# A decoder layer on one core: a new opening, a buffer moved, and a new table of order offsets

## The chip, the core and the metric

The kernel runs on one NeuronCore of a Trainium2 chip. The core has a matrix engine (TensorE; PE in the profile, with its weight loads shown apart as PEld), a vector engine (VectorE, DVE), a scalar engine for activations and copies (ScalarE, ACT), a general engine (GpSimd, POOL) and a queue engine that here only issues transfers (SyncE, SP). Each engine executes its own list of instructions strictly in the order of that list and waits at its head for what it needs. ScalarE and GpSimd can issue transfers as well. Matrix products write to PSUM; everything else lives in SBUF. The metric is device time in microseconds (us) of the whole program; 1557.06 us is the median of three runs before the change, and lower is better.

## What is computed

A decoder layer in float32 for 4 sequences (B) of 512 tokens and width 512, in three parts, each followed by "add to the residual and layer-normalise":

```
x = layernorm(x + attention(x))   # 8 differential heads: p1 - lam * p2, 4 key/value groups, causal
x = layernorm(x + mamba(ctx) )    # in-projection of a 256-wide context, 4-tap convolution, silu,
                                  # x-projection to dt/B/C, a scan of 16 states over 512 steps, times silu(x)
x = layernorm(x + ffn(x))         # shared gated unit + 16 experts in a latent of 128, top 8 of 16 weighted
```

The second part's in-projection, convolution, x-projection and scan depend only on the context `ctx`, so they can run from the beginning beside the attention. The feed-forward part first projects the tokens to the 128-wide latent (`xl`) and to 16 gate values, and every expert is computed for every token with a weight that may be zero.

## The kernel before

**Who orders the work.** The body does not issue instructions at once. Every `nc.<engine>.<op>` call is recorded by `Notes.note` (L208) as a step with a key, a time-like number: a stage's own due time (`nc.key`) plus an offset from the table `SHIFT` (L23 to L39), looked up by the name of the tile written and the initial of the engine ("y.v": the tile `y` on VectorE; "cT.s": the tile `cT` from SyncE or ScalarE). When all is recorded, `Notes.order` (L253) plays the program through once with fixed costs per step: whenever an engine is free in that play, it takes the ready step with the lowest key. A step is only taken if its buffer is free, and VectorE operations that read two SBUF operands are kept apart in time from wide GpSimd additions. `Notes.trace` emits the steps in the order found, all from one line, so that nearly every row of the profile says L358. The order is thus fixed before the run; if on the chip an input comes later than in that play, the engine waits even if later steps of its list could run.

**The opening.** L455 to L475 load, all from SyncE's queue: small vectors (`bq`, `cw`, `cb`), the in-projection weights `w_in` in two halves and the first sequence's context `cT0` in two halves, then `xT0` (the transposed tokens), the first key, query and value weights (`wk`, `wq`, `wv`), `w_xp`, the lambda vectors `lt`, and more small ones. With key 0, L477 to L487 turn the lambda vectors into `nlam` (tiles `lp`, `ls`) and `a_neg` into its negated exponential on VectorE and ScalarE. L490 to L496 load the four residuals `res[b]` (1 MB each) and the output bias `obb`, and let GpSimd add `obb` to each residual, one 128 by 2048 addition for each sequence.

**The context part.** `scan(b)` (L647) has four products of two steps each into `ps_in` (8 products; a float32 product is two MATMUL records in the trace, so 16 records), a copy of each to `xm`, one ScalarE and three VectorE operations of the convolution into `y`, a sigmoid `sgc` on ScalarE over each pair of blocks, and `y * sgc` on VectorE. `ps_x` needs both halves of `y`; its copy `xd` goes out to memory, comes back as broadcast rows `bc`, and feeds products `ps_dt` with only 16 rows of weights. Then come 16 state steps of two halves with a scan instruction each, accumulated to memory by GpSimd's transfers `y<-h`. For the first sequence all of this has key 0; `ps_qk`, `ps_v` and `s` products of the first attention unit follow.

**Attention and experts.** 16 attention units (4 groups by 4 sequences), each with about 73.8 us of key. Then `experts(b)` for each sequence: gate and latent products `ps_gate`, `xr` (the latent by tokens, copied from PSUM by ScalarE), four transposes `pt_l` into `xl`, the top-8 weights, the shared unit (`pg_s`, `ph_s`), and 16 experts of `pg`, `ph`, `pa`, fed by `wb`, `xw` and `ht`, two buffers each. SBUF tiles come from tagged sets: "pT" has 2 buffers and "c2" has 6 (`C2`). `wb`, `xw`, `ht` are all from "c2", as are `w_in`, `xm`, `xd`, `w_dt` earlier on; `xr`, `wT`, `aT`, `sg` and `relu_s` are from "pT".

Of the kernel before, what the change touches and what calls it, by code (L numbers as in the profile page):

```python
# [19 lines left out]
P = 128  # L20
ENGINES = ("tensor", "vector", "scalar", "gpsimd", "sync")

SHIFT = {  # L23
    "aT.s": 15.4, "a_neg.s": 12.1, "a_neg.v": -7.8, "bc.s": 7.4, "bq.s": -3.3, "bvb.s": -2.6, "cT.s": -3.5,
    "cf.v": -1.7, "cw.s": -2.2, "da.g": -4.8, "da.s": -1, "db.s": 4.2, "dsk.s": 2.1, "dt.s": -2.1, "dt.v": -7.7,
    "du.v": 21.2, "e.s": 7.6, "e.v": -2.1, "gb.s": -1.2, "h.v": -4.3, "ht.v": -6.5, "kT.s": 3.9, "l.v": 2.1,
    "ln_mv.v": -14.5, "ln_nb.v": -33.8, "ln_rs.g": -2.5, "ln_st.v": 4.7, "ln_ve.v": -21.4, "lo.v": 12.6, "lp.v":
    2.2, "ls.s": -1.8, "ls.v": -6.6, "lt.s": 3, "m.v": -3.7, "ms.v": -4.3, "nlam.v": -8.1, "o.s": -12.8, "oT.s":
    0.7, "obb.s": 17, "ow.s": -1.2, "pT.s": -2.7, "pa.t": 1, "pg.t": -2.1, "pg_s.t": -8.4, "ph.t": 2.8, "ph_s.t":
    3.2, "po.t": -7.2, "pr.s": -9.5, "pr.v": -13, "ps_dt.t": -0.1, "ps_gate.t": -18.9, "ps_in.t": -1.8,  # L30
    "ps_out.t": 5.1, "ps_qk.t": 1.3, "ps_v.t": 2.1, "ps_x.t": 12.8, "ps_y.t": 2.9, "pt.t": -0.3, "pt_o.t": 2.7,
    "pt_w.t": -7.1, "pt_x.t": 1.5, "pt_y.t": -5.9, "qT.s": 0.6, "relu.s": 20.5, "relu_s.s": -3.8, "res.g": -0.4,
    "res.s": -5.4, "res.v": -1.8, "rp.v": -16.4, "rs.g": 6.5, "rs.v": -12.2, "s.t": 0.9, "sc.v": 4, "sg.s": -1.5,
    "sg.v": 4.3, "sgc.s": 3.9, "sh.v": 7.5, "sp.v": 15.5, "sq.s": -16.2, "sub.s": -33.5, "sub.v": -9.9, "v.v":
    1.5, "w.s": 6.4, "wT.s": -1.1, "w_dg.s": 0.9, "w_dt.s": 6.5, "w_e.s": 23.5, "w_in.s": -30.8, "w_s.s": -0.3,
    "w_u.s": -4.7, "w_xp.s": 1.8, "wb.s": 10.2, "wq.s": 2.4, "wv.s": 5.9, "x2T.s": -13.1, "xd.s": 17.9, "xl.s":
    2.9, "xm.g": 1.7, "xm.s": 7.8, "xr.s": -1, "xw.v": 3.9, "y.g": -4.6, "y.s": 7.9, "y.v": -9.9, "yb.s": 5.6,
    "yb.v": 2.7,
}  # L39
B, S, HID = 4, 512, 512  # L40
NT = S // P
# [3 lines left out]
CTX, DI, NST, DTR, KC = 256, 512, 16, 16, 4  # L45
ND = DI // P
LAT, FH, NE, SCALE = 128, 256, 16, 2.5
NEG = -1e30
C2 = 6
# [322 lines left out]
def decoder_kernel(  # L372
# [11 lines left out]
    sb = Pool(ctx.enter_context(tc.tile_pool(name="sb", bufs=1)))  # L384
    ps = Pool(ctx.enter_context(tc.tile_pool(name="ps", bufs=1, space=PSUM)), psum=True)
    dram = Pool(ctx.enter_context(tc.tile_pool(name="scratch", bufs=1, space=DRAM)))

    ident = fixed.tile([P, P], F32, tag="ident", name="ident")
# [10 lines left out]
    nc = Notes(real)  # L399

    def load(shape, src, tag, name=None, bufs=1, most=0):
        t = sb.tile(shape, tag, name or tag, bufs, most)
        nc.sync.dma_start(out=t, in_=src)
        return t

    def small(shape, tag, bufs=8):
        return sb.tile(shape, tag, tag, bufs)
# [35 lines left out]
    def load_q(g):  # L443
        return [
            load([P, 4, 256], wqkvT[:, k : k + 256].rearrange("(c p) n -> p c n", p=P), "wq", "wq", 2)
            for k in (g * 512, g * 512 + 256)
        ]
# [4 lines left out]
    def load_cT(b):  # L452
        return load([P, 2, S], ctxT[b].rearrange("(c p) t -> p c t", p=P), "h", "cT", 5)

    nc.key = -40.0  # L455
    bq = load([P, 32], bqkv, "bq")
    cw = load([P, ND, KC], convw, "cw")
    cb = load([P, ND], convb, "cb")
    w_in, cT0 = [], sb.tile([P, 2, S], "h", "cT", 5)
    for c in range(2):  # L460
        w_in.append(load([P, DI], inT[c * P : (c + 1) * P, :], "c2", "w_in", C2))
        nc.sync.dma_start(out=cT0[:, c, :], in_=ctxT[0, c * P : (c + 1) * P, :])
    xT0 = sb.tile([P, 4, S], "t8", "xT")
    wk0 = load_k(0)
    for c in range(4):
        nc.sync.dma_start(out=xT0[:, c, :], in_=xT[0, c * P : (c + 1) * P, :])
    wq0 = load_q(0)
    wv0 = load_v(0)
    w_xp = load([P, ND, 48], xpT.rearrange("(c p) n -> p c n", p=P), "w_xp")
    lt = load([P, 2, 2, HD], lam4.partition_broadcast(P).rearrange("p (a c d) -> p a c d", a=2, c=2), "qT", "lt", 2)  # L470
    sub = load([P, 2], subln, "sub")
    w_dt = load([DTR, DI], dtT, "c2", "w_dt", C2)
    db = load([P, ND], dtb, "db")
    dsk = load([P, ND], dskip, "dsk")
    a_neg = load([P, ND, NST], alog, "a_neg")  # L475
# [4 lines left out]
    lp = sb.tile([P, 2, HD], "o", "lp", 2)  # L480
    ls = sb.tile([P, 2], "ls")
    nlam = sb.tile([P, 1], "nlam")
# [8 lines left out]
    res = [sb.tile([P, NT, HID], f"res{b}") for b in range(B)]  # L491
    obb = load([P, HID], ob.partition_broadcast(P), "oT", "obb", 2)
# [13 lines left out]
    def layernorm(src, dst, tiles=range(NT)):  # L506
        st = small([P, NT, 6], "ln_st", 2)
        mv = small([P, NT, 2], "ln_mv", 2)
        ve = small([P, NT], "ln_ve", 2)
        rs = small([P, NT], "ln_rs", 2)  # L510
        nb = small([P, NT], "ln_nb", 2)
        k = slice(tiles[0], tiles[-1] + 1)
        for i in tiles:
            nc.vector.bn_stats(out=st[:, i, :], in_=src[:, i, :])
            nc.vector.bn_aggr(out=mv[:, i, :], in_=st[:, i, :])
        nc.vector.tensor_scalar(ve[:, k], mv[:, k, 1], EPS, None, ALU.add)
        nc.gpsimd.tensor_tensor(rs[:, k], ve[:, k], mhalf[:, k], ALU.pow)
        nc.vector.scalar_tensor_tensor(nb[:, k], mv[:, k, 0], -1.0, rs[:, k], ALU.mult, ALU.mult)
        for i in tiles:
            nc.scalar.activation(  # L520
                dst[:, i, :], src[:, i, :], AF.Identity, bias=nb[:, i : i + 1], scale=rs[:, i : i + 1]
            )


    qk_scale = HD ** -0.5
# [204 lines left out]
    w_dg = sb.tile([P, 4, LAT + NE], "w_dg")  # L730
    nc.sync.dma_start(out=w_dg[:, :, :LAT], in_=wdT.rearrange("(c p) n -> p c n", p=P))
    nc.sync.dma_start(out=w_dg[:, :, LAT:], in_=wgT.rearrange("(c p) n -> p c n", p=P))
    gb = load([P, NE], gbias.partition_broadcast(P), "gb")
    w_s = sb.tile([P, 2, 4, FH], "t8", "w_s")
# [3 lines left out]
    w_u = load([P, HID], wuT, "wq", "w_u", 2)  # L738
# [6 lines left out]
    def experts(b):  # L745
        T = t_expert(b)
        nc.key = T - LEAD[b]
        if b:
            yb = [load([P, 2, S], y_d[b][:, k : k + 2, :], "o", "yb", 2) for k in (0, 2)]
            yb = [yb[d // 2][:, d % 2, :] for d in range(ND)]  # L750
        else:
            yb = [load([P, S], y_d[b][:, d, :], "c2", "yb", C2, 4) for d in range(ND)]
        nc.key = max(T - LEAD[b] + 10.0, nc.key + 5.0)
        for i in range(NT):
            sg = sb.tile([P, HID], "pT", "sg", 2)
# [3 lines left out]
        for i in range(NT):  # L759
            pt = ps.tile([P, S], "tr", "pt_y", 1)  # L760
# [4 lines left out]
        x2T = [sb.tile([P, 2, S], t, "x2T") for t in ("wk", "wv")]  # L765
        x2T = [x2T[c // 2][:, c % 2, :] for c in range(4)]
        for c in range(4):
            pt = ps.tile([P, S], "tr", "pt_x", 1)
# [3 lines left out]


        nc.key += 10.0
        pls, xr = [], sb.tile([P, NT, LAT], "pT", "xr", 2)
        for k in range(2):
            pl = ps.tile([P, 2, 256], "mm", "ps_gate", 3)
            for i in range(2):
                t = 2 * k + i
                for c in range(4):  # L780
                    nc.tensor.matmul(
                        pl[:, i, : LAT + NE], lhsT=x2T[c][:, t * P : (t + 1) * P], rhs=w_dg[:, c, :],
                        start=(c == 0), stop=(c == 3),
                    )
            pls.append(pl)
        pr = small([P, NT, NE], "pr", 1)
# [4 lines left out]
        pt = ps.tile([P, S], "tr", "pt_l", 1)  # L791
        for i in range(NT):
            nc.tensor.transpose(pt[:, i * P : (i + 1) * P], xr[:, i, :], ident)
        xl = sb.tile([P, S], "kT", "xl", 2)
        nc.scalar.copy(xl, pt)
        sc = small([P, NT, NE], "sc", 1)
        nc.vector.tensor_tensor(sc, pr, gb.repeat(1, [P, NT, NE]), ALU.add)
        m8 = small([P, NT, 8], "m8", 1)
        rp = small([P, NT, NE], "rp", 1)
        for i in range(NT):  # L800
            nc.vector.max(out=m8[:, i, :], in_=sc[:, i, :])
            nc.vector.match_replace(
                out=rp[:, i, :], in_to_replace=m8[:, i, :], in_values=sc[:, i, :], imm_value=-3e38
# [3 lines left out]
        sp = small([P, NT], "sp", 2)  # L807
# [3 lines left out]
        pt = ps.tile([P, S], "tr", "pt_w", 1)  # L811
        for i in range(NT):
            nc.tensor.transpose(pt[:NE, i * P : (i + 1) * P], pr[:, i, :], ident)
        wT = sb.tile([NE, S], "pT", "wT", 2)
# [5 lines left out]
        sh = sb.tile([P, 2, S], "v", "sh", 2)  # L820
        for k in range(2):
            pg = ps.tile([P, S], "s", "pg_s", 3)
            for c in range(4):
                nc.tensor.matmul(
                    pg, lhsT=w_s[:, 0, c, k * P : (k + 1) * P], rhs=x2T[c], start=(c == 0), stop=(c == 3)
                )
            ph = ps.tile([P, S], "s", "ph_s", 3)
            for c in range(4):
                nc.tensor.matmul(
                    ph, lhsT=w_s[:, 1, c, k * P : (k + 1) * P], rhs=x2T[c], start=(c == 0), stop=(c == 3)  # L830
# [4 lines left out]
        pa = ps.tile([P, S], "po", "pa") if b else ps.tile([P, S], "mm", "pa", 3)  # L835
        for e in range(NE):
            nc.key = t_expert(b, e) - WEIGHTS
            w_e = sb.tile([P, 3, FH], "w_e", "w_e", 4)
# [3 lines left out]
            wb = sb.tile([P, S], "c2", "wb", C2, 2)  # L842
            nc.sync.dma_start(out=wb, in_=w_dr[b].row(e))
            nc.key = t_expert(b, e) - SCALED
            xw = sb.tile([P, S], "c2", "xw", C2, 2)
            nc.vector.tensor_tensor(xw, xl, wb, ALU.mult)
            for k in range(2):
                nc.key = t_expert(b, e + 0.5 * k)
                pg = ps.tile([P, S], "s", "pg", 3)
                nc.tensor.matmul(pg, lhsT=w_e[:, 0, k * P : (k + 1) * P], rhs=xl, start=True, stop=True)  # L850
                ph = ps.tile([P, S], "mm", "ph", 3)
                nc.tensor.matmul(ph, lhsT=w_e[:, 1, k * P : (k + 1) * P], rhs=xw, start=True, stop=True)
                ht = sb.tile([P, S], "c2", "ht", C2, 2)
# [3 lines left out]
                    pa, lhsT=w_e[:, 2, k * LAT : (k + 1) * LAT], rhs=ht,  # L857
                    start=(e == 0 and k == 0), stop=(e == NE - 1 and k == 1),
                )
        nc.key = t_expert(b, NE) + 4.0  # L860
        aT = sb.tile([P, S], "pT", "aT", 2)
        nc.scalar.copy(aT, pa)
        for i in range(NT):
            po = ps.tile([P, HID], "mm", "ps_y", 3)
            nc.tensor.matmul(po, lhsT=aT[:, i * P : (i + 1) * P], rhs=w_u, start=True, stop=False)
            for k in range(2):
                nc.tensor.matmul(
                    po, lhsT=sh[:, k, i * P : (i + 1) * P], rhs=w_s2[:, k, :], start=False, stop=(k == 1)
# [9 lines left out]
    for b in range(B):  # L878
        experts(b)
# [64 lines left out]
```

## Time and profile before

| what | value |
|---|---|
| runs | 1556.51, 1557.06, 1564.02 us |
| profiled execution, its own time | 1558.77 us |
| its span, first to last instruction | 1557.0 us |
| PE busy | 1534.4 us (99%), 4928 MATMUL records |
| DVE busy | 1204.0 us (77%) |
| ACT busy | 953.2 us (61%) |
| POOL busy | 193.9 us (12%) |
| mean granted TensorE clock | 0.992 |

The span is what the profile divides up; 1.8 us of the profiled execution's time lie around it. A busy PE need not be a fast one: the granted clock can be half, and the same product then takes twice as long. The lists of waits say, for each engine, what ended the time it stood idle.

### The profile page before, as it was taken

What the parts mean: (1) busy time and instruction counts of PE and PEld (TensorE: products, weight loads), DVE (VectorE), ACT (ScalarE), POOL (GpSimd) and SP (SyncE); (2) the same over time, 40 slices, a digit from 0 to 9 for tenths busy, and PEclk for the clock granted to TensorE, in tenths of its full rate; (3) what the DMA queues carried; (4) which work ended last, traced back from release to release, by engine and by line L of the source; (5) the groups of instructions that cost most, each with busy time, mean ns of one, the idle gap of its engine ahead of it and who ended that gap; (6) DMA issues with size and microseconds to landing.
All of it is one profiled execution on the core that took longest, in us unless ns stands there. A gap on an engine that the chain in (4) does not pass through costs nothing.

```text
span 1557.0 us, 15843 instructions
## 1 busy us (share of the span) xinstructions
PE 1534.4 (99%) x4928; PEld 846.0 (54%) x4928; DVE 1204.0 (77%) x2036; ACT 953.2 (61%) x2096; POOL 193.9 (12%) x208
## 2 busy tenths in 40 slices
PE   7999999999999999999999999999999999999998
PEld 2665665655656566565655555555545445445443
DVE  6559998777999887888988989999999962534433
ACT  3586566566756656576656658676967553444343
POOL 4011121101111111111111021211111100000000
PEclk9999999999999999999999999999999999999999
DMA  7126676525467763646765555665776851541341
GB/s 266 55 68 117 123 157 143 127 59 119 81 135 158 150 123 88 128 87 127 178 144 114 107 116 119 128 165 112 179 170 138 196 168 55 159 129 61 117 126 49
DMA packets 105523, 196.18 MB, mean 126 GB/s; under 512 B 10896, under 2 KB 45712, under 8 KB 105440
## 3 DMA queue, kind: packets, MB, share of 16 engines
q1 hardware_dynamic: 87008, 128.06, 29.1%
q0 software_dynamic: 18432, 67.12, 25.0%
q8 instruction: 39, 0.64, 0.2%
q14 instruction: 44, 0.36, 0.1%
HBM read 119.25 MB, written 75.89 MB: 125 GB/s over the span
## 4 chain that ended last, share of the span: by engine, by line
PE 96%; DVE 3%; ACT 0%; DMA 0%; issue 0%; SPq 0%; POOLq 0%; ACTq 0%
PE ps_qk L358 21%; PE ps_out L358 14%; PE s L358 9%; PE po L358 9%; PE ps_v L358 7%; PE pa L358 7%; PE ph L358 7%; PE pg L358 7%; PE ps_y L358 3%; PE pt L358 2%; PE pg_s L358 2%; PE ph_s L358 2%; PE pt_o L358 2%; PE ps_in L358 2%; PE ps_dt L358 1%; PE ps_gate L358 1%
## 5 line engine op out<-in xcount | busy, mean ns | idle before, releaser
L358 DVE TENSOR_TENSOR_SCAN h<-da,h 128x1024 f32<-128x1024 f32 x128 | 292.7, 2286 | 2.9 <-ACT da L358 0.4
L358 PE MATMUL ps_qk<-xT,wq 128*128 128x512 f32 x512 | 242.2, 594 | 0.0
L358 PE MATMUL ps_out<-ow,oT 128*128 128x512 f32 x512 | 238.1, 596 | 0.0
L358 POOL DMA_DIRECT2D y<-h x128 | 111.6, 872 | 795.1 <-DVE h L358 568.5
L358 ACT ACTIVATE da<-dt,a_neg 128x512 f32<-128x512 f32 (+1 forms) x256 | 175.1, 716 | 29.9 <-DVE h L358 25.9
L358 DVE TENSOR_TENSOR ht<-relu,ph 128x512 f32<-128x512 f32 x128 | 87.6, 685 | 125.3 <-PE ph L358 91.8
L358 ACT ACTIVATE relu<-pg 128x512 f32<-128x512 f32 x128 | 76.0, 593 | 160.4 <-PE pg L358 160.0
L358 PE MATMUL s<-kT,qT 128*128 128x384 f32 (+3 forms) x512 | 169.8, 440 | 1.1 <-DVE nm L358 1.1
L358 DVE CUSTOM_DVE_ANT_0 e<-s,mask 128x128 f32<-128x128 f32 (+3 forms) x256 | 118.9, 485 | 54.7 <-PE s L358 50.9
L358 PE MATMUL po<-v,pT 128*128 128x256 f32 x640 | 160.3, 381 | 0.4 <-ACT pT L358 0.4
L358 ACT ACTIVATE e<-e,nm 128x128 f32<-128x128 f32 (+3 forms) x256 | 142.0, 557 | 28.2 <-DVE nm L358 27.1
L358 DVE TENSOR_TENSOR h<-h,bc 128x1024 f32<-128x1024 f32 x128 | 156.2, 1220 | 1.3
L358 DVE TENSOR_TENSOR h<-du,bc 128x1024 f32<-128x1024 f32 x128 | 155.9, 1218 | 0.1
L358 PEld LDWEIGHTS po<-v,pT 128*128 128x128 f32 x640 | 121.7, 191 | 61.9 <-issue 35.2
L358 PEld LDWEIGHTS ps_out<-ow,oT 128*128 128x128 f32 x512 | 93.9, 192 | 83.7 <-issue 78.9
L358 PEld LDWEIGHTS ps_qk<-xT,wq 128*128 128x128 f32 x512 | 92.3, 191 | 77.3 <-issue 70.1
L358 PE MATMUL pa<-ht,w_e 128*128 128x512 f32 x256 | 130.8, 593 | 0.1
L358 PE MATMUL ph<-xw,w_e 128*128 128x512 f32 x256 | 130.3, 592 | 0.0
L358 PE MATMUL pg<-xl,w_e 128*128 128x512 f32 x256 | 129.4, 592 | 0.0
L358 PEld LDWEIGHTS s<-kT,qT 128*128 128x128 f32 x512 | 88.8, 192 | 63.5 <-issue 48.7
L358 PE MATMUL ps_qk<-xT,wk 128*128 128x512 f32 x256 | 120.9, 592 | 0.0
L358 ACT ACTIVATE sq<-po 128x256 f32<-128x256 f32 x128 | 48.7, 381 | 115.4 <-PE po L358 114.6
(121 smaller groups left out, 2084.0 us busy)
## 6 DMA issues: line engine op xcount, KB each, us to landing
y<-h POOLq DMA_DIRECT2D x128, 512.0 KB, 7.9
bc<-bc SPq DMA_DIRECT2D x64, 512.0 KB, 6.3
wb<-w SPq DMA_DIRECT2D x64, 256.0 KB, 3.4
xT<-in_xT_dram SPq DMA_DIRECT2D x15, 1024.0 KB, 7.8
w_e<-in_rwgT_dram SPq DMA_DIRECT2D x64, 128.0 KB, 2.2
w_e<-in_rw1T_dram SPq DMA_DIRECT2D x64, 128.0 KB, 2.3
w_e<-in_rw2T_dram SPq DMA_DIRECT2D x64, 128.0 KB, 2.5
wq<-in_wqkvT_dram SPq DMA_DIRECT2D x8, 512.0 KB, 5.9
```

Source lines behind the costliest of these rows:

```text
L358: getattr(getattr(self.nc, s.engine), s.name)(*[get(a) for a in s.args], **{k: get(v) for k, v in s.kw.items()})
```

## The change

Three edits and a new table of offsets.

- The opening's keys are split: the two halves of `w_in` and of `cT0` get -60, `cw` and `cb` -50, and `bq` moves behind the `xT0` loads at -40. The two `cT0` transfers are issued by ScalarE (`nc.scalar.dma_start`) instead of SyncE.
- Eight products of the 128 by 128 identity with itself, with key -60, into a PSUM tile `warm` of the tag "tr" that nothing reads.
- `xr` in `experts` is taken from "c2" (at most one at a time) instead of "pT".
- All of `SHIFT` is replaced. Six names are new in it: `cb.s`, `du.s`, `pt_l.t`, `warm.t`, `wk.s`, `xT.s`.

```diff
 SHIFT = {
-    "aT.s": 15.4, "a_neg.s": 12.1, "a_neg.v": -7.8, "bc.s": 7.4, "bq.s": -3.3, "bvb.s": -2.6, "cT.s": -3.5,
-    "cf.v": -1.7, "cw.s": -2.2, "da.g": -4.8, "da.s": -1, "db.s": 4.2, "dsk.s": 2.1, "dt.s": -2.1, "dt.v": -7.7,
...
-    2.2, "ls.s": -1.8, "ls.v": -6.6, "lt.s": 3, "m.v": -3.7, "ms.v": -4.3, "nlam.v": -8.1, "o.s": -12.8, "oT.s":
-    0.7, "obb.s": 17, "ow.s": -1.2, "pT.s": -2.7, "pa.t": 1, "pg.t": -2.1, "pg_s.t": -8.4, "ph.t": 2.8, "ph_s.t":
-    3.2, "po.t": -7.2, "pr.s": -9.5, "pr.v": -13, "ps_dt.t": -0.1, "ps_gate.t": -18.9, "ps_in.t": -1.8,
...
-    2.9, "xm.g": 1.7, "xm.s": 7.8, "xr.s": -1, "xw.v": 3.9, "y.g": -4.6, "y.s": 7.9, "y.v": -9.9, "yb.s": 5.6,
+    "aT.s": 14.5, "a_neg.s": 24.2, "a_neg.v": -20.6, "bc.s": 7.7, "bq.s": -13.6, "bvb.s": 10.1, "cT.s": 5.3,
+    "cb.s": 8.3, "cf.v": 3, "cw.s": -23.6, "da.g": -3.2, "da.s": -5.2, "db.s": 10.3, "dsk.s": -4.9, "dt.s": -1.3,
...
+    "kT.s": 12.3, "l.v": 4.2, "ln_mv.v": 0.1, "ln_nb.v": -25.4, "ln_rs.g": -10.3, "ln_st.v": 3.6, "ln_ve.v": 1,
+    "lo.v": 8.9, "lp.v": 43.7, "ls.s": 5.2, "ls.v": -24.7, "lt.s": 4.8, "m.v": 14, "ms.v": -5, "nlam.v": -10.2,
+    "o.s": -25.7, "oT.s": -3, "obb.s": 11.9, "ow.s": 18.5, "pT.s": -2.4, "pa.t": 1.2, "pg.t": -2.1, "pg_s.t":
+    -8.5, "ph.t": 2.9, "ph_s.t": 6.7, "po.t": -2, "pr.s": -32.2, "pr.v": -30.1, "ps_dt.t": -7.8, "ps_gate.t":
+    -12.7, "ps_in.t": -2.4, "ps_out.t": 5.2, "ps_qk.t": -0.8, "ps_v.t": 3, "ps_x.t": -7.7, "ps_y.t": 23, "pt_l.t":
+    -12.3, "pt_o.t": 3.5, "pt_w.t": -22.5, "pt_x.t": 0.2, "pt_y.t": -4.2, "qT.s": -3, "relu.s": 2.7, "relu_s.s":
+    -16, "res.g": -7.1, "res.s": 8.6, "res.v": -5.4, "rp.v": -15.7, "rs.g": -8.4, "rs.v": -6.7, "s.t": 0.9,
...
+    "sub.v": -15.2, "v.v": -7.6, "w.s": -18, "wT.s": -0.2, "w_dg.s": 1.7, "w_dt.s": 55.1, "w_e.s": 27, "w_in.s":
+    -33.7, "w_s.s": -13.3, "w_u.s": 17, "w_xp.s": 2.8, "warm.t": 4.2, "wb.s": 18, "wk.s": -16.8, "wq.s": 7.9,
+    "wv.s": 8.9, "x2T.s": -8.7, "xT.s": 1.8, "xd.s": 30.3, "xl.s": 4.6, "xm.g": 22.4, "xm.s": 3.4, "xr.s": -1.7,
+    "xw.v": 6.8, "y.g": -13.9, "y.s": 7.8, "y.v": -40.6, "yb.s": -4.2, "yb.v": -5.7,
 }
...
-    nc.key = -40.0
-    bq = load([P, 32], bqkv, "bq")
-    cw = load([P, ND, KC], convw, "cw")
-    cb = load([P, ND], convb, "cb")
+    nc.key = -60.0
     w_in, cT0 = [], sb.tile([P, 2, S], "h", "cT", 5)
     for c in range(2):
         w_in.append(load([P, DI], inT[c * P : (c + 1) * P, :], "c2", "w_in", C2))
-        nc.sync.dma_start(out=cT0[:, c, :], in_=ctxT[0, c * P : (c + 1) * P, :])
+        nc.scalar.dma_start(out=cT0[:, c, :], in_=ctxT[0, c * P : (c + 1) * P, :])
+    nc.key = -50.0
+    cw = load([P, ND, KC], convw, "cw")
+    cb = load([P, ND], convb, "cb")
+    nc.key = -40.0
     xT0 = sb.tile([P, 4, S], "t8", "xT")
     wk0 = load_k(0)
     for c in range(4):
         nc.sync.dma_start(out=xT0[:, c, :], in_=xT[0, c * P : (c + 1) * P, :])
+    bq = load([P, 32], bqkv, "bq")
...
+    nc.key = -60.0
+    pw = ps.tile([P, S], "tr", "warm", 1)
+    for i in range(8):
+        nc.tensor.matmul(pw[:, :P], lhsT=ident, rhs=ident, start=True, stop=True)
...
-        pls, xr = [], sb.tile([P, NT, LAT], "pT", "xr", 2)
+        pls, xr = [], sb.tile([P, NT, LAT], "c2", "xr", C2, 1)
```

More of the change, by code (lines that the diff above doesn't have):

```diff
@@ L23 @@
 SHIFT = {
-    "aT.s": 15.4, "a_neg.s": 12.1, "a_neg.v": -7.8, "bc.s": 7.4, "bq.s": -3.3, "bvb.s": -2.6, "cT.s": -3.5,
-    "cf.v": -1.7, "cw.s": -2.2, "da.g": -4.8, "da.s": -1, "db.s": 4.2, "dsk.s": 2.1, "dt.s": -2.1, "dt.v": -7.7,
-    "du.v": 21.2, "e.s": 7.6, "e.v": -2.1, "gb.s": -1.2, "h.v": -4.3, "ht.v": -6.5, "kT.s": 3.9, "l.v": 2.1,
-    "ln_mv.v": -14.5, "ln_nb.v": -33.8, "ln_rs.g": -2.5, "ln_st.v": 4.7, "ln_ve.v": -21.4, "lo.v": 12.6, "lp.v":
-    2.2, "ls.s": -1.8, "ls.v": -6.6, "lt.s": 3, "m.v": -3.7, "ms.v": -4.3, "nlam.v": -8.1, "o.s": -12.8, "oT.s":
@@ L29 @@
-    0.7, "obb.s": 17, "ow.s": -1.2, "pT.s": -2.7, "pa.t": 1, "pg.t": -2.1, "pg_s.t": -8.4, "ph.t": 2.8, "ph_s.t":
-    3.2, "po.t": -7.2, "pr.s": -9.5, "pr.v": -13, "ps_dt.t": -0.1, "ps_gate.t": -18.9, "ps_in.t": -1.8,
-    "ps_out.t": 5.1, "ps_qk.t": 1.3, "ps_v.t": 2.1, "ps_x.t": 12.8, "ps_y.t": 2.9, "pt.t": -0.3, "pt_o.t": 2.7,
-    "pt_w.t": -7.1, "pt_x.t": 1.5, "pt_y.t": -5.9, "qT.s": 0.6, "relu.s": 20.5, "relu_s.s": -3.8, "res.g": -0.4,
-    "res.s": -5.4, "res.v": -1.8, "rp.v": -16.4, "rs.g": 6.5, "rs.v": -12.2, "s.t": 0.9, "sc.v": 4, "sg.s": -1.5,
@@ L34 @@
-    "sg.v": 4.3, "sgc.s": 3.9, "sh.v": 7.5, "sp.v": 15.5, "sq.s": -16.2, "sub.s": -33.5, "sub.v": -9.9, "v.v":
-    1.5, "w.s": 6.4, "wT.s": -1.1, "w_dg.s": 0.9, "w_dt.s": 6.5, "w_e.s": 23.5, "w_in.s": -30.8, "w_s.s": -0.3,
-    "w_u.s": -4.7, "w_xp.s": 1.8, "wb.s": 10.2, "wq.s": 2.4, "wv.s": 5.9, "x2T.s": -13.1, "xd.s": 17.9, "xl.s":
-    2.9, "xm.g": 1.7, "xm.s": 7.8, "xr.s": -1, "xw.v": 3.9, "y.g": -4.6, "y.s": 7.9, "y.v": -9.9, "yb.s": 5.6,
-    "yb.v": 2.7,
+    "aT.s": 14.5, "a_neg.s": 24.2, "a_neg.v": -20.6, "bc.s": 7.7, "bq.s": -13.6, "bvb.s": 10.1, "cT.s": 5.3,
@@ new lines @@
+    "cb.s": 8.3, "cf.v": 3, "cw.s": -23.6, "da.g": -3.2, "da.s": -5.2, "db.s": 10.3, "dsk.s": -4.9, "dt.s": -1.3,
+    "dt.v": 9.5, "du.s": 0.1, "du.v": 29, "e.s": 10.2, "e.v": -3.2, "gb.s": -9.6, "h.v": -4.8, "ht.v": -0.1,
+    "kT.s": 12.3, "l.v": 4.2, "ln_mv.v": 0.1, "ln_nb.v": -25.4, "ln_rs.g": -10.3, "ln_st.v": 3.6, "ln_ve.v": 1,
+    "lo.v": 8.9, "lp.v": 43.7, "ls.s": 5.2, "ls.v": -24.7, "lt.s": 4.8, "m.v": 14, "ms.v": -5, "nlam.v": -10.2,
+    "o.s": -25.7, "oT.s": -3, "obb.s": 11.9, "ow.s": 18.5, "pT.s": -2.4, "pa.t": 1.2, "pg.t": -2.1, "pg_s.t":
@@ new lines @@
+    -8.5, "ph.t": 2.9, "ph_s.t": 6.7, "po.t": -2, "pr.s": -32.2, "pr.v": -30.1, "ps_dt.t": -7.8, "ps_gate.t":
+    -12.7, "ps_in.t": -2.4, "ps_out.t": 5.2, "ps_qk.t": -0.8, "ps_v.t": 3, "ps_x.t": -7.7, "ps_y.t": 23, "pt_l.t":
+    -12.3, "pt_o.t": 3.5, "pt_w.t": -22.5, "pt_x.t": 0.2, "pt_y.t": -4.2, "qT.s": -3, "relu.s": 2.7, "relu_s.s":
+    -16, "res.g": -7.1, "res.s": 8.6, "res.v": -5.4, "rp.v": -15.7, "rs.g": -8.4, "rs.v": -6.7, "s.t": 0.9,
+    "sc.v": 7.3, "sg.s": -2, "sg.v": 3.3, "sgc.s": 0.3, "sh.v": -3.2, "sp.v": 21.3, "sq.s": 6.5, "sub.s": -29.8,
```

## The prediction

> **What bounds the kernel.** I read the page's chain first, then PE's own waits, then the time order of the first 40 us, then stretches with their granted clock.
>
> ```profile
> PE 96%; DVE 3%; ACT 0%; DMA 0%; issue 0%; SPq 0%; POOLq 0%; ACTq 0%
> ```
>
> TensorE sets the end. It is busy for 1534.4 of 1557.0 us, so 22.6 us are idle. Its own waits show where (total, times, longest):
>
> ```profile
> PE ps_in L358 <- DMA cT<-in_ctxT_dram: 5.9, 1, 5.9
> PE ps_x L358 <- DVE y L358: 5.3, 1, 5.3
> PE s L358 <- DVE nm L358: 1.1, 2, 0.6
> ```
>
> Two waits, both in the first 33 us, make 11.1 us (5.86 and 5.25). After the last product, at about 1550.05, some 7 us of layer norm and store follow. What is left, 22.6 - 11.1 - 7 = 4.5 us, is spread over the middle (2.9 of it in 1040 to 1060). So outside the opening nearly nothing is to be had from idle time. In order of time:
>
> ```profile
> 2.12 0.91 SPq L358 DMA_DIRECT2D cT<-in_ctxT_dram  x2
> 5.86 9.10 PE L358 MATMUL ps_in<-cT,w_in 128*128 128x512 f32 x16 [5.86 <-DMA cT<-in_ctxT_dram]
> ...
> 22.26 19.07 POOL L358 TENSOR_TENSOR res<-res,obb 128x2048 f32<-128x2048 f32 x4 [7.49 <-DMA obb<-in_ob_dram]
> 22.30 4.76 DVE L358 TENSOR_TENSOR lp<-lt 128x256 f32<-128x256 f32 x1
> ...
> 27.10 0.42 DVE L358 TENSOR_REDUCE ls<-lp 128x2 f32<-128x256 f32 x1
> 27.43 5.07 DVE L358 TENSOR_TENSOR y<-y,sgc 128x1024 f32<-128x1024 f32 x1
> ...
> 32.55 3.65 PE L358 MATMUL ps_x<-y,w_xp 128*48 128x512 f32 x4 [5.25 <-DVE y L358]
> ```
>
> The second wait has a cause worth seeing. The first product y*sgc took 1.22 us (at 18.93); the second took 5.07. The small lp took 4.76 us. Both fell while GpSimd added obb to the residuals (four additions of about 4.6 us, back to back from 22.26), and the two engines took turns: lp behind the first addition, y behind the second. The scalar engine's sigmoid was ready at 23.5; y came at 32.50. The third loss is the clock:
>
> ```profile
> 30.00:35.00 5.00, 2.44 (x3) 0.64 (x4) 5.00 (x2) 0.00 (x0) 5.00 (x2) 0.54 0.36 133
> 376.00:384.00 8.00, 8.00 (x15) 3.83 (x15) 5.33 (x8) 4.67 (x10) 0.86 (x1) 0.63 0.55 133
> 660.00:666.00 6.00, 6.00 (x14) 3.61 (x15) 3.67 (x7) 5.95 (x11) 0.80 (x1) 0.56 0.77 153
> ```
>
> (Stretch, busy time and count of PE, PEld, DVE, ACT, POOL, then granted clock, DMA share, GB/s.) The clock is at half from about 30.3 to 37.2, begun by the idle stretch; the work from 32.55 on runs in it, so it costs (37.2 - 32.55) / 2 = 2.3 us on top of the 5.25. Around 376 to 384 and 660 to 666 the clock is halved with no idle time, beside the 16-row products ps_dt; (1 - 0.63) x 8 plus 0.46 from the two microseconds before is 3.4 us, and the other is 3.4 us by the same sum. At the start, five records step by 0.85 us instead of 0.43 until full speed at about 9.9: 2 us. I use 0.5% (7.8 us) as what a measurement of this kernel can tell from no change.
>
> **Part 1, the start.** The new keys put w_in's two halves first on SyncE (issues at 0.74 and 1.19 in place of sub's 0.74 and their own 1.19) and cT0's two on ScalarE, whose list has nothing else before its copy at 10.70 but a table load, 0.74 to 2.02. Before, the first context half was issued at 2.12 and landed 3.6 us later, at 5.7, behind 0.5 MB of weights. Bytes flow from about 2.6 (1.4 us after w_in's issue) at 300 to 390 GB/s; half a megabyte, the first pair, is through at about 3.8 in the new order, and with the same 0.7 us to its completion lands near 4.5. If the issues stand behind the table load, cT0 goes out at 2.02 and lands where it did, 5.6. [...]
>
> [...] A product of the code is two records (8 in-projection products are the 16 records above). A 128-column record steps by 0.11 us at full clock and by 0.21 at half (pt, two records in 0.38 us and in 0.63 us). Identity is ready at 1.70 (GpSimd's row, 1.41 + 0.29), so 16 records run from about 1.85 to 1.85 + 16 x 0.213 = 5.26. In-projection starts at 5.3 whether its data came at 4.5 or 5.3; at 5.6 in the bad case. What the products buy is the clock. The row: full speed came 4.0 us after the first record (5.86 to 9.86), which now is 5.85. [...] I take 6.4. Then the records step 5.3, 6.15, 6.8 and from there by 0.43; the 17th starts at 6.8 + 14 x 0.43 = 12.8 instead of 14.79: **2.0 us earlier**. [...] A loss here I exclude: even fully cold it starts before 5.86. [...]
>
> The small loads move. bq, bvb go behind the big ones, first needed at 18.6 and 42: hidden. w_dt falls behind a_neg, needed at 59: hidden by 40 us. cb is now about eighth on SyncE: issued near 3.9, landed near 7.2 to 8.6 by its 3.3 us and the half megabyte of wk ahead; ScalarE wants it at about 8.7. If 1 us late, the convolution slides 1 us, within the slack below.
>
> **Part 2, the second y.** VectorE's chain up to y shifts with the in-projection by 2.0: lp from 22.30 to 20.3, the second sigmoid's end from 23.48 to 21.5. The residual additions need res[0] and obb, which have the same 5.8 MB ahead as before; with the flow starting 0.45 us earlier they begin near 21.8 instead of 22.26. So the operation that was 0.04 us too late before, lp, now has 1.5 us in hand, and y has 0.3. The offsets push the same way: y.v goes from -9.9 to -40.6, lp.v from 2.2 to 43.7, so where both are ready y goes first. TensorE has other work until 27.30 - 2.0 = 25.3. Three outcomes: y starts ahead of GpSimd, ends at 22.7 and no wait is left: **7.55 us** gained (5.25 + 2.3). [...] Or lp is caught first and y behind the next one: the wait stays about as long as it is, and nothing is gained here. lp's near tie decides, and the shift is three times as large on VectorE as on GpSimd; I take the first. Where the additions go: they end near 41 in either case; the first reader of res is the output sum after 115, so they are late for nobody. nlam and a_neg, the next two-operand operations, wait behind the later additions as before (to 41.38), which v's sum at 42.10 did not feel.
>
> **Part 3, xr in "c2".** The copy is 0.37 us, two for each sequence; xr is held from 1064.4 to 1069.4, 5 us, four times. In "pT" it stood beside relu_s and wT; ScalarE's waits tied to relu_s sum to a few us and TensorE waited for none of them. In "c2" it joins wb, xw, ht, which may fill all six buffers. Best case +2 us; worst, one expert step of 5.15 us lost each time, since the copy at the head of ScalarE's list holds relu behind it, and pg, ph, pa wait for relu: 20.6. I take 0, as wb is sent well ahead (its landing took 3.4 us, and VectorE waited for it 2.1 us in all).
>
> **Part 4, all other offsets.** They reorder everything and can't be costed line by line. From the rows: the best they can do is remove the 4.5 us of scattered idle time and both 3.4 us half-clock stretches, 11.3 us. The worst is more of the same: two more such stretches (four scans have ps_dt, two lost the clock; ps_dt.t from -0.1 to -7.8 may cluster them), 6.8 us, and waits like the 2.9 us one. The offsets of the large products hardly move (s 0.9 to 0.9, pg -2.1 to -2.1, ps_out 5.1 to 5.2, ph 2.8 to 2.9). I take 0.
>
> **Sum.** 2.0 + 7.55 = 9.55 off a span of 1557.0: 1547.5. The profiled execution's own time is 1558.77, 1.8 around the span, and becomes 1549.2. The median of the runs, 1557.06, lies 1.7 below that execution, so the gain taken off it gives **1547.5 us**; its own range, from the ends of part 1, 1544 to 1551.
>
> **Rivals.** *One addition in the way:* y loses its 0.3 us lead. For: the lead is smaller than the spread of any landing; against: y's lower key. [...] *The collision stays:* the bytes flow more smoothly, obb lands by 20 and lp is caught again; the change then does only its opening. For: res and obb are now neighbours in the list, and obb no longer straggles (it took 7.9 us). 1557.06 - 2.0 = 1555. [...] *Slower:* "c2" runs dry at the gate of each sequence; at 5.15 us x 4 = 20.6 against 9.55 gained that is 1568. It decides once the wait is over (9.55 + 7.8) / 4 = 4.3 us at each gate. Against it: 5 us of holding must fall wholly into a moment when all six are taken; for it: relu, ht and TensorE are in step there (each expert's records follow one another without a gap), so nothing absorbs a lost buffer.
>
> **How the numbers follow.** No wait 0.36, one addition 0.20, collision stays 0.18, middle improves 0.09, slower 0.17. Below 1549.3 (faster by over 0.5%) lie 0.29 of the first, 0.09 of the second and the fourth: 0.47. Slower by over 0.5%: 0.17. The rest, 0.36, is within. From 1541 to 1564 lie the first three, half of the fourth and some of the slower case: 0.8.
>
> **What would show it.** Right: 16 records of warm from about 1.9, ps_in at 5.3, full clock by 6 to 9; y's second product at 1.2 us; no PE wait before ps_x; no half clock near 30. Part 3 wrong: ScalarE or VectorE waiting at xr, xw or wb, and PE idle in 1180 to 1440. Part 4 wrong: new PE waits or half-clock stretches after 60. The forecast fails if y still stands behind an addition, or if idle time in the middle grows by more than 4 us.

## The result and the profile after

| | before | changed |
|---|---|---|
| median of 6 runs each | 1556.99 us (1555.96 to 1564.29) | 1542.67 us (1541.55 to 1544.28) |
| profiled execution, its span | 1557.0 us | 1542.0 us |
| PE busy | 1534.4 us | 1528.2 us |
| mean granted TensorE clock | 0.992 | 0.998 |

The changed kernel takes 0.9895 of the time before (95% interval 0.9871 to 0.9919): it is about 14.3 us faster, where 9.5 were forecast. In the profiles the difference is 15.0 us.

First TensorE's own waits in the changed kernel (total, times, longest). Neither of the two waits that made 11.1 us before is left; the start's wait is now for the identity, 1.8 us.

```profile
PE po L358 <- ACT pT L358: 1.9, 2, 1.6
PE pt_y L358 <- DVE res L358: 1.8, 2, 1.0
PE warm L358 <- POOL ident masks.py:199: 1.8, 1, 1.8
```

Then the opening in order of time (start, duration, engine, what). Both context transfers go out at 0.74 beside the weights, and ScalarE's table load comes after them. The in-projection starts at 5.33 and the first attention product at 12.63 (14.79 before). On VectorE all twelve convolution steps stand ahead of both y products; lp takes 0.42 us and the second y 1.23, and GpSimd's first addition begins 0.9 us after that y has started. The x-projection follows without a wait.

```profile
0.74 0.89 ACTq L358 DMA_DIRECT2D cT<-in_ctxT_dram  x2
1.66 1.28 ACT L358 ACT_TABLE_LOAD   x1 [1.66 <-PEq L940]
1.75 3.78 PE L358 MATMUL warm<-ident 128*128 128x128 f32 x16 [1.75 <-POOL ident masks.py:199]
5.33 7.47 PE L358 MATMUL ps_in<-cT,w_in 128*128 128x512 f32 x16
12.63 7.03 PE L358 MATMUL ps_qk<-xT,wk 128*128 128x512 f32 x16
...
21.89 0.42 DVE L358 TENSOR_TENSOR lp<-lt 128x256 f32<-128x256 f32 x1
22.26 1.23 DVE L358 TENSOR_TENSOR y<-y,sgc 128x1024 f32<-128x1024 f32 x1
23.03 3.63 PE L358 MATMUL ps_x<-y,w_xp 128*48 128x512 f32 x8
23.15 18.13 POOL L358 TENSOR_TENSOR res<-res,obb 128x2048 f32<-128x2048 f32 x4 [9.01 <-DMA res<-in_x_dram]
```

By 37.04 the changed kernel has done what the kernel before had done at 47.08 (both then start the first `s` product, after the same number of in-projection, attention and x-projection products): 10.04 of the 15.0 us. The other 5 lie in the middle: from there to the end of the last product it is 1502.97 us before and 1498.04 now, though TensorE's idle time in it went from 4.5 to 5.1 us. The stretches with their clock show where they come from (stretch; busy time and count of PE, PEld, DVE, ACT, POOL; clock, DMA share, GB/s):

```profile
355.00:360.00 5.00, 5.00 (x13) 2.13 (x12) 3.09 (x6) 3.58 (x12) 0.92 (x1) 1.00 0.44 75
360.00:365.00 5.00, 5.00 (x14) 2.83 (x13) 1.00 (x4) 2.94 (x7) 0.00 (x0) 0.66 0.87 246
365.00:370.00 5.00, 5.00 (x19) 2.35 (x18) 3.09 (x11) 4.05 (x8) 0.00 (x0) 1.00 0.57 167
```

Between 40 and the last layer norm, this is the only half-clock stretch of the changed kernel: (1 - 0.66) x 5 = 1.7 us of clock lost. The kernel before had two of 3.4 us. 6.8 - 1.7 = 5.1.

### The profile page after: what moved, and what is told of

It reads as the page before. It is cut to its first block, busy times and chain, and to the rows that moved or that the text cites. A ratio compares the mean times of both kernels' runs of the same rounds, so it can differ in the third digit from the quotient of the medians.

```text
span 1542.0 us, 15795 instructions
## 1 busy us (share of the span) xinstructions
PE 1528.2 (99%) x4944; PEld 846.3 (55%) x4944; DVE 1194.9 (77%) x2036; ACT 950.7 (62%) x2092; POOL 194.6 (13%) x208
## 4 chain that ended last, share of the span: by engine, by line
PE 98%; DVE 1%; ACT 1%; issue 0%; POOL 0%; POOLq 0%; DVEq 0%
PE ps_qk L358 21%; PE ps_out L358 14%; PE po L358 9%; PE s L358 9%; PE ps_v L358 7%; PE pa L358 7%; PE ph L358 7%; PE pg L358 7%; PE ps_y L358 3%; PE pt L358 2%; PE pt_o L358 2%; PE ps_in L358 2%; PE pg_s L358 2%; PE ph_s L358 2%; PE ps_dt L358 1%; PE ps_gate L358 1%
## 5 line engine op out<-in xcount | busy, mean ns | idle before, releaser
L358 PE MATMUL ps_qk<-xT,wq 128*128 128x512 f32 x512 | 238.5, 593 | 0.0
L358 PE MATMUL s<-kT,qT 128*128 128x384 f32 (+3 forms) x512 | 164.7, 436 | 0.0
L358 PE MATMUL ps_v<-wv,xT 128*128 128x256 f32 x512 | 118.6, 380 | 0.0
```

The lines of the kernel that those rows point to most:

```text
L358: getattr(getattr(self.nc, s.engine), s.name)(*[get(a) for a in s.args], **{k: get(v) for k, v in s.kw.items()})
```

## The experiments

A VectorE operation that is caught behind an addition, or not, moves a run by about 10 us (9.2 us of span in the run with early additions below), and some of these kernels sit close to that border: their runs fall into groups, and the kernel before, timed again beside each set, has medians of 1557.3, 1560.4 and 1559.1 us. A profile shows one run of such a group, so each reading below names both, the profile's rows and the spread of the times. The changed kernel itself, run again:

> The changed kernel once more, beside the others of this group, since its runs fell on two values (1541.6 and 1543.7) that lie 2.1 us apart. [...] Rival (another chip is simply slower): the kernel before moves by the same share.

It took 1544.08 us (1543.81 to 1544.49), 0.9916 of the kernel before (0.9886 to 0.9945); span 1542.2, with the same single stretch near 361. The kernel before stayed where it was (1557.3 for 1556.99), so nothing speaks for a slower chip. These six runs all lie near 1544, the earlier ones near 1541.6 and 1543.7. The profiles suggest what parts them. Two profiled runs near 1544 (1543.76 and 1543.96) have their stretch near 361. Two near 1541.7 are of variants below, context by SyncE (1541.81) and xr in pT (1541.64), and have theirs at 917 to 920. There it comes just before a place where TensorE otherwise waits 1.6 us for pT, and that wait is then gone: this stretch costs next to nothing.

**Do the additions decide the wait?** Two loads moved in SyncE's list, and nothing else: in the kernel before a residual and obb behind ow, so that the additions start later; in the changed kernel obb and the first residual ahead of wv, so that they start earlier.

```diff
 # kernel before: order of SyncE's list
-    res, obb, res, ow, res, res
+    res, ow, res, obb, res, res
 # changed kernel: order of SyncE's list
-    wv, bvb, db, a_neg, w_dt, obb, res0
+    obb, res0, wv, bvb, db, a_neg, w_dt
```

> The kernel before, with the loads of one residual and of obb moved behind the load of ow in SyncE's list, and nothing else: GpSimd's additions can start only some 3 to 5 us later. Theory (the additions catch lp and y): lp takes 0.4 us, the second y about 1.2, TensorE's 5.25 us wait before ps_x is gone and with it the half clock near 30: 1549 to 1551. Rival (the wait comes from the order or from late loads of the weights): the wait stays and the time is 1556 to 1558.

> The changed kernel with the loads of obb and the first residual moved ahead of wv in SyncE's list, and nothing else, so that GpSimd's additions can start about 2 us earlier (near 21). Theory: an addition begins before lp at 21.9 or before the second y at 22.26; one or both wait 4 us each, ps_x comes 2 to 7 us late, and 2 to 9 us are lost with the clock: 1545 to 1552. Rival (the new order of VectorE alone made the wait go): no PE wait before ps_x, time within 0.5 us.

The kernel before with late additions, VectorE's and GpSimd's rows in order of time:

```profile
23.25 0.42 DVE L363 TENSOR_TENSOR lp<-lt 128x256 f32<-128x256 f32 x1
...
24.46 1.23 DVE L363 TENSOR_TENSOR y<-y,sgc 128x1024 f32<-128x1024 f32 x1 [0.33 <-ACT sgc L363]
...
27.73 17.94 POOL L363 TENSOR_TENSOR res<-res,obb 128x2048 f32<-128x2048 f32 x4 [12.01 <-DMA obb<-in_ob_dram]
28.18 1.92 PE L363 MATMUL ps_x<-y,w_xp 128*48 128x512 f32 x4
```

The wait before ps_x is gone, as is the half clock near 30; the span is 1548.0 although its start was later (in-projection at 6.30). Not all of the 9.0 us between 1557.0 and 1548.0 is the wait: this profile also lost 3.4 us instead of 6.8 to half clock in the middle. Timed, it took 1555.21 us (1549.75 to 1558.43), 0.9966 (0.9947 to 0.9985). The sign is as the theory says, the size in the median is smaller than in the profile. The changed kernel with early additions:

```profile
21.08 19.60 POOL L363 TENSOR_TENSOR res<-res,obb 128x2048 f32<-128x2048 f32 x4 [7.13 <-DMA res<-in_x_dram]
21.69 4.73 DVE L363 TENSOR_TENSOR lp<-lt 128x256 f32<-128x256 f32 x1
26.34 5.51 DVE L363 TENSOR_TENSOR y<-y,sgc 128x1024 f32<-128x1024 f32 x1
31.90 3.65 PE L363 MATMUL ps_x<-y,w_xp 128*48 128x512 f32 x4 [7.15 <-DVE y L363]
```

The changed kernel's order, and the wait is back, 7.15 us, with a half-clock stretch after it; 1553.42 us (1541.54 to 1557.54), span 1551.4, 9.2 over the 1542.2 of the run beside it, just over the upper end of the 2 to 9 us expected. Eight of its ten runs lie above 1553, two at 1541.5 and 1544.4. The rival, that the order of VectorE alone did it, falls: the same order loses 9 us when the additions start 2.1 us earlier (21.08 for 23.15).

**Is it the opening's edits, or the table?** The table of offsets alone in the kernel before, and the opening with the old table.

```diff
 # kernel before, the table alone
-SHIFT = { ... the old values ... }
+SHIFT = { ... the new values ... }
 # changed kernel, the table alone undone
-SHIFT = { ... the new values ... }
+SHIFT = { ... the old values ... }
```

> The kernel before with the new table of offsets alone: no identity products, context by SyncE, old keys of the opening, xr in pT. Theory: the order of the opening and the later start of the additions come with the offsets, so the wait before ps_x (5.25) and its half clock (2.3) are gone or shrink to one addition, and what the start brings (2.2) is not: 1544 to 1550. Rival (it is the earlier start that pulls y ahead of the additions): the wait stays, 1553 to 1558.

> The changed kernel with the old table of offsets (the opening's loads and keys, the identity products and xr in c2 stay). Theory of the prediction (the earlier start pulls lp and y ahead of the additions): VectorE's old order stays, lp runs near 20.3 and the second y at 21.5, ahead of additions near 21.8 to 22.3; the start's 2 us and the 7.5 of the wait are gained, 1547 to 1549, with the half-clock stretches of the middle as before; in some runs an addition comes first and the time is 5 to 9 us longer. Rival (the new offsets' later loads of res are needed): lp is caught in most runs, 1554 to 1558.

Both expectations for the table alone fell: it is slower than the kernel before, 1562.49 us (1561.36 to 1565.53), 1.0026 (1.0013 to 1.0040). Its list of TensorE's waits:

```profile
PE ps_v L358 <- DVE v L358: 9.6, 1, 9.6
PE ps_qk L358 <- DMA xT<-in_xT_dram: 8.3, 1, 8.3
```

Without the opening's keys the new offsets put xT and wk ahead of the context. Attention goes first, waits 8.3 us for its tokens, the convolution comes so late that the additions catch its own steps (nine took 23.43 us from 22.24), and v stands behind them. On this kernel the table is good only with the opening it came with.

The opening with the old table took 1553.62 us (1548.74 to 1560.48), 0.9968 (0.9953 to 0.9983). Its rows in order of time are the forecast's case without collision, and have the numbers the prediction gave for it (lp at 20.3, y at 21.5, additions near 21.8):

```profile
20.30 0.42 DVE L358 TENSOR_TENSOR lp<-lt 128x256 f32<-128x256 f32 x1
...
21.50 1.22 DVE L358 TENSOR_TENSOR y<-y,sgc 128x1024 f32<-128x1024 f32 x1 [0.34 <-ACT sgc L358]
22.07 18.45 POOL L358 TENSOR_TENSOR res<-res,obb 128x2048 f32<-128x2048 f32 x4 [9.31 <-DMA obb<-in_ob_dram]
```

So the earlier start does pull y ahead in this profile, with 0.57 us in hand, without any new offset. But the span is 1549.9 and most runs miss the 1547 to 1549 expected, since the middle is slow; whether an addition came first in some of them no profile shows. Its stretches with their clock:

```profile
50.00:60.00 10.00, 10.00 (x21) 4.36 (x21) 5.49 (x17) 6.56 (x15) 0.00 (x0) 0.66 0.34 111
365.00:377.00 12.00, 12.00 (x22) 4.92 (x21) 5.95 (x8) 6.55 (x13) 0.86 (x1) 0.57 0.59 145
650.00:658.00 8.00, 8.00 (x22) 4.04 (x22) 5.11 (x12) 6.89 (x11) 0.86 (x1) 0.79 0.62 104
```

That is 3.4 + 5.2 + 1.7, about 10.2 us lost to the clock, against 1.7 in the changed kernel. Here the table earns its keep.

**What halves the clock in the middle?** The step products ps_dt on 96 rows (the added weights are zero), with the x-projection on 96 columns to give them 96 valid rows; on both kernels. And the x-projection alone (the edit is shortened here).

```diff
-    w_xp = load([P, ND, 48], ...)
+    w_xp = sb.tile([P, ND, 96], ...)   # zeros, columns 0 to 47 loaded
-    w_dt = load([DTR, DI], ...)
+    w_dt = sb.tile([96, DI], ...)      # zeros, rows 0 to 15 loaded
-    px[:48, :] ... rhs=xd[:DTR, :]
+    px[:96, :] ... rhs=xd              # xd has 96 rows
```

> The changed kernel with the step products ps_dt on 96 rows instead of 16 (the added rows of weights are zero, the added rows of the other operand come from a wider x-projection of 96 columns instead of 48, also zero there), so the output is the same; order unchanged. Theory (few rows make the clock drop): no half-clock stretch between the opening and the last layer norm, 1.7 us for each stretch window gone, 1540 to 1542. Rival (short waits around these products make it drop): the stretch near 361 stays and the time is the same within 0.5 us.

> The kernel before with ps_dt on 96 rows instead of 16 and the x-projection on 96 columns instead of 48 (all added weights zero), order unchanged. Theory (few rows make the clock drop): the half-clock stretches at 375 to 382 and 656 to 663 are gone, 3.4 us each: about 1550; the one at 30 to 37, which idle time begins, stays. Rival (waits do it): both stay, 1556 to 1558.

> The changed kernel with only the x-projection widened to 96 columns (zeros added, only the first 48 rows of its output used); ps_dt stays on 16 rows; order unchanged. Both widened gained 6.8 us in the profiles, of which 1.7 is the half-clock stretch near 361. Theory (each step between products of unlike shape costs TensorE 0.3 to 0.5 us, and few rows drop the clock): the part at ps_x, about 1.5 to 2 us, is gained, the stretch stays: 1541.5 to 1542.5 beside 1544. Rival (all of it hangs on the 16 rows): no gain, 1543.5 to 1544.5.

The stretches of the middle with their clock, first of the kernel before:

```profile
360.00:380.00 20.00, 20.00 (x57) 9.61 (x56) 14.20 (x24) 13.54 (x33) 3.66 (x4) 0.88 0.66 143
640.00:660.00 20.00, 20.00 (x59) 9.41 (x58) 16.46 (x28) 10.43 (x27) 1.77 (x3) 0.96 0.60 146
```

The same two stretches of the kernel before with 96 rows:

```profile
360.00:380.00 20.00, 20.00 (x66) 11.27 (x65) 17.30 (x29) 15.82 (x39) 4.18 (x4) 1.00 0.67 149
640.00:660.00 20.00, 20.00 (x64) 10.89 (x64) 18.14 (x29) 13.25 (x29) 1.70 (x2) 1.00 0.57 108
```

The busy time is the same 20 us, but 57 records became 66, and 59 became 64. No stretch is left in the middle of either kernel with 96 rows, while the one near 32 that idle time begins stayed in the kernel before. It took 1547.32 us (0.9913, 0.9887 to 0.9938), the changed kernel 1536.55 us (0.9865, 0.9823 to 0.9907), faster than both kernels of this case. With only the x-projection widened the stretch at 360.6 stays (clock 0.66 in 360 to 365): 1540.89 us. The granted clock of every run agrees: all four of the padded kernel before show 0.997 and all four of the padded changed kernel 0.999, where the kernel before has 0.988 to 0.996 in 91 of the 92 runs timed beside these sets and the changed kernel 0.998 in all twelve. So the half clock of the middle needs the 16-row products. Plain waits did not bring it: a wait of 1.8 us at po stayed with 96 rows, and the clock stayed up. One thing is not set apart: padding also removed short unfilled steps beside these products, as follows.

Both gained more than expected. Laid record by record beside the changed kernel, the 96-row kernel pulls ahead at every ps_x and ps_dt, not only at the stretch: 6.8 us in all (1542.2 to 1535.4). The clock of the middle gave 1.7; its start was 0.7 us worse (first attention product at 13.51 for 12.82, full clock coming later), so the products gave about 5.8. A block of six ps_dt records, TensorE's rows in order of time (start, duration), in the changed kernel:

```profile
358.64 3.00 PE L358 MATMUL ps_dt<-xd,w_dt 16*128 16x512 f32 x6
```

And in the changed kernel with 96 rows:

```profile
357.33 2.74 PE L358 MATMUL ps_dt<-xd,w_dt 96*128 96x512 f32 x6
```

With the x-projection alone the span is 2.7 us shorter (1542.2 to 1539.5), 0.5 of it at the start (12.36 for 12.82): about 2.2 us are the products', just above the 1.5 to 2 expected. The cost of a single step is smaller than the 0.3 to 0.5 us of that theory: in the changed kernel's trace the step from ps_qk to ps_x, or from ps_x to what follows it, takes 0.52 us, one within ps_x 0.43 or 0.47.

**The parts of the opening one by one**, each taken from the changed kernel with the order of all else kept: the identity products; the context by ScalarE; both.

```diff
 # without the identity products
-    nc.key = -60.0
-    pw = ps.tile([P, S], "tr", "warm", 1)
-    for i in range(8):
-        nc.tensor.matmul(pw[:, :P], lhsT=ident, rhs=ident, start=True, stop=True)
 # context by SyncE: changed where the steps are emitted, so that the order stays
-            getattr(getattr(self.nc, s.engine), s.name)(
+            engine = "sync" if s.name == "dma_start" else s.engine
+            engine = s.engine if s.engine == "gpsimd" else engine
+            getattr(getattr(self.nc, engine), s.name)(
```

> The changed kernel without the eight identity products; every engine's order of the other instructions is the same. Theory: in-projection starts at about 4.5 instead of 5.33, but at half clock until about 4.0 us later (8.5 to 9.6); the first attention product starts at 13.3 to 14.2 instead of 12.63, and 0.7 to 1.6 us are lost, 1543 to 1545 against 1541.6 to 1543.7. Rival (the products only stand in the way, loads set the start): the first attention product comes no later than 12.63 and the time is the same or up to 0.8 us shorter.

> The changed kernel with the two context transfers issued by SyncE, in the places of its list where the order puts them (context, weights, context, weights); all other instructions keep their order. Theory: two issues of 0.43 us are added ahead of the first pair's completion, the pair lands by about 5 and the identity products cover it; 0 to 0.5 us lost. Rival (ScalarE's queue is what makes the opening fast): in-projection waits for its data to 5.8 and more, 0.7 to 1.5 us lost.

> The changed kernel without the identity products and with the context issued by SyncE. Each alone cost 0.2 us or less at the start. Theory (the two cover for each other only in the start's first microsecond; keys alone bring the rest): in-projection starts at 4.6 to 5.2, the first attention product at 13.0 to 13.9, 0.4 to 1.3 us after the changed kernel's, and the second y comes near 22.7 to 23.5, so that an addition catches it in many runs: these lie 9 to 11 us higher, the others at 1543 to 1545. Rival (the edits of the opening beside the offsets bring nothing): first attention product by 12.8 and no run above 1546.

| kernel | in-projection starts | full clock from | first attention product | second y's lead over the additions | runs |
|---|---|---|---|---|---|
| changed | 5.33 | 6.18 | 12.63 | 0.89 | 1541.6 to 1544.5 (12) |
| no identity products | 4.41 | 7.39 | 12.85 | 0.66 | 1542.8 to 1544.6 (12), 1550.1 to 1554.9 (8) |
| context by SyncE | 5.33 | 5.57 | 12.33 | 2.00 | 1541.4 to 1544.4 (6) |
| neither | 4.29 | 8.62 | 13.39 | 0.70 | 1542.5 to 1547.4 (9) |

The in-projection without the identity products ahead of it, first with the context by ScalarE, then by SyncE:

```profile
4.41 8.60 PE L358 MATMUL ps_in<-cT,w_in 128*128 128x512 f32 x16 [4.41 <-DMA cT<-in_ctxT_dram]
```

```profile
4.29 9.26 PE L360 MATMUL ps_in<-cT,w_in 128*128 128x512 f32 x16 [4.29 <-DMA w_in<-in_inT_dram]
```

Without the identity products, in-projection began 0.9 us earlier in half clock and the first attention product was late by just 0.22, less than the 0.7 expected: full speed came 3.0 us after the first record there. One pair of profiles can't size this, since the moment of full clock moves by more from run to run. In the eight profiles that have the identity products, all starting at 1.75, full clock comes between 4.75 and 7.96 and the first attention product between 11.93 and 13.51; the two without have 12.85 and 13.39. What does differ is the runs: eight of the twenty without them are 7 to 11 us longer, and none of the changed kernel's twelve. The likely reading is that in those an addition came first; no profile of such a run was taken. The rival, that the products stand in the way, is not borne out.

Moving the context to ScalarE brought nothing that shows: the data are there at 4.41 by ScalarE and at 4.29 by SyncE, and 12.33 against 12.63 is when full clock was granted. Without both, 0.76 us are lost at the first attention product, as expected, but only one of nine runs is slower than 1546, and by 2 us; the additions start at 23.71 in its profile. The leads in the table are of one profile each (the changed kernel's other profile has 1.71), so they don't say why.

**xr.** Back in pT:

```diff
-        pls, xr = [], sb.tile([P, NT, LAT], "c2", "xr", C2, 1)
+        pls, xr = [], sb.tile([P, NT, LAT], "pT", "xr", 2)
```

> The changed kernel with xr back in pT (ten rows of TensorE's order and twelve of ScalarE's differ, all in the experts). Theory: nothing on the critical path, 1541.5 to 1545. Rival (pT was short at the gates): 1 to 3 us lost, with waits of ScalarE or TensorE at relu_s, wT or sg.

1543.87 us (1541.64 to 1544.29) beside 1544.08: nothing. TensorE's waits are those of the changed kernel but for the 1.6 us one at po, which is missing here. That is not xr's doing: with the context by SyncE and xr in c2 it is missing too. Both profiles have their half-clock stretch just before it, at 917 to 920.

## Why the prediction was right or wrong, point by point

- **What bounds the kernel:** right. Nearly all that could be had lay in the opening and in the clock, and it came from there.
- **Part 1, the start, 2.0 us:** right in sum, 2.16 measured (14.79 to 12.63). In-projection at 5.33 for 5.3, full clock at 6.18 for 6.4. The credit was off: 1.4 us of it came by the order of the loads alone (14.79 to 13.39 in the one profile without the other two). What the identity products add is within the spread of when full clock comes, and the move to ScalarE added none: with both transfers in SyncE's list, in-projection still started at 5.33, because the identity products covered it, and without them at 4.29 against 4.41. So the forecast's 4.5 for the first pair was right, and no run shows data as late as its 5.3: by either engine they were there by 4.4. The 6.4 for full clock was the author's choice, and no run shows a source for it, nor for the ends of this part in the range: in the profiles with the identity products full clock came anywhere between 4.75 and 7.96. The 4.0 us taken from one row for the clock's delay ran from 3.0 (4.41 to 7.39) to 6.2 (1.75 to 7.96): it is not one constant. In the traces of both kernels every change of the clock lies a whole multiple of 3.41 us after its first rise: 6, 8, 107, 109, 190, 192 and 452 times before, 104, 105 and 449 times in the changed kernel.
- **Part 2, the second y, 7.55 us:** right; to 37.04 against 47.08 it is 10.04 less 2.16, 7.9. The collision is shown from both sides, by delaying the additions and by advancing them. The working that gave it (lp 20.3, y 21.5, additions 21.8) holds for the opening with the old table, to 0.3 us. In the changed kernel itself both sides are elsewhere: y at 22.26, since all convolution steps and the first y now precede it, and the additions at 23.15, since they wait for the residual's load instead of obb. With additions at the forecast's 21.8, lp at 21.89 would have come second, as in the run with additions at 21.08. That was luck: a true result by a different margin. (The shift of lp against that of the additions, 2.0 to 0.46, is also more than the three times that the text says.)
- **Part 3, xr, 0 us:** right.
- **Part 4, all other offsets, taken as 0:** this is the step that failed. The middle became 4.9 us shorter, and the granted clock accounts for it (5.1 us, while idle time grew by 0.6). The bound had it (both half-clock stretches, 6.8 us), and what the chances call "middle improves", at 0.09, is what came true for the most part: without both stretches the forecast would have been 1547.5 - 6.8 = 1540.7. That they need the 16-row products is shown. That the new order makes fewer of them is seen, not taken apart: in the middle, the three profiles with the old table and 16 rows (before, late additions, old table) lost 6.8, 3.4 and 10.2 us to half clock, the nine with the new table between 0 and 3.4, 1.7 in the mean (the table alone lost 5.1 more behind its wait of 9.6 us, which is idle time and not counted here). ps_dt's lower offset, feared in the text as a source of more stretches, went with fewer.

The traces say more of how. In the third sequence the eight ps_dt records stand within 5.6 us before and in two blocks 7 us apart in the changed kernel:

```profile
654.31 1.98 PE L358 MATMUL ps_dt<-xd,w_dt 16*128 16x512 f32 x4
656.63 1.12 PE L358 MATMUL ps_dt<-xd,w_dt 16*128 16x512 f32 x2
658.10 1.80 PE L358 MATMUL ps_dt<-xd,w_dt 16*128 16x512 f32 x2
```

```profile
629.14 1.98 PE L358 MATMUL ps_dt<-xd,w_dt 16*128 16x512 f32 x4
636.15 1.98 PE L358 MATMUL ps_dt<-xd,w_dt 16*128 16x512 f32 x4
```

Cut each trace into stretches of 3.41 us from the first rise of the clock, and add up in each the time from every ps_dt record to the record after it. In the twelve profiles with 16 rows the clock fell 15 times with no idle time before it, each time at the end of a stretch with 2.08 to 2.77 us of ps_dt (2.08 and 2.58 in the kernel before, 2.55 in the changed one). It stayed up after 123 stretches with at most 1.96 us, and after four with 2.06 to 2.31. With 96 rows it stayed up even after 2.49 and 2.58 us. So both seem to matter: how close together the order puts these products, which the new table changed, and where the 3.41 us begin. The second is the author's reading of why the changed kernel's own order, in the variants above, lost anything from 0 to 3.4 us. This is a count over traces; no run moved ps_dt alone.

The slower rival did not come: no product of TensorE is listed as waiting for xr, xw or wb, and VectorE waited 2.6 us in all at xw (2.1 before).

## What to carry to other kernels

Where GpSimd and VectorE share work with two operands in SBUF, look for near ties: here additions that started 2 us earlier cost 9 us, and delaying two loads that nobody needed yet removed the wait in the profile. When a new table of priorities can't be costed line by line, look at what the old order loses without being idle: here the granted clock, which cost 6.8 us where TensorE's idle time in the middle was 4.5. Products of few rows can be worth padding with zeros: here that, with the 48-column products padded too, took 10.6 us off the span of the kernel before and 6.8 off the changed one, with TensorE's order as it was.

## What the runs showed of the hardware that had not been expected

- The clock fell to half with TensorE busy throughout, beside products of 16 rows, and not when the same products had 96 rows (11 of 12 profiles against none of 2). The stretches last 3.4, 6.8 or 10.2 us: 6.83 us from 375.10 and from 658.40 in the kernel before, 3.41 from 361.19 in the changed one, and about 10.2 between 365 and 377 with the old table.
- A half-clock stretch need not cost its half: the one at 917 to 920 only filled a wait of 1.6 us that stands behind it otherwise.
- Narrow products cost time beyond the clock: about 5.8 us over 32 ps_dt and 32 ps_x records and their neighbours, at full clock, went when they were widened to 96 rows and columns, though a single record is no shorter (0.59 us in both).
- On this kernel, GpSimd's and VectorE's two-operand work took turns one operation at a time, even when the VectorE operation has one column: in the kernel before lp, y and nlam took 4.76, 5.07 and 4.45 us beside additions of 4.5 to 5.5 us, and in the changed one nlam took 4.52 us, where it is 0.16 us without an addition beside it. It is not only two-operand work: a_neg's step, which reads one tensor (the forecast counts it with the two-operand ones), took 4.40 us before and 0.18 with late additions.
